# Attention block and two quantised convolutions in one kernel: a new tail for the depthwise stage, and the order of work around four stage borders

## The chip, the core and the metric

The kernel runs on one core of a Trainium2 chip. The metric is the device time of one execution in microseconds (us). Engines are written as in the profile: PE (TensorE matmul), PEld (its weight loads), DVE (VectorE), ACT (ScalarE), POOL (GpSimd), SP (SyncE, which here only issues DMAs). Lines such as L684 are lines of the kernel before; lines of the changed kernel are called so where they are used.

## What is computed

The input x is 4 images of 128 channels and 128 x 128 pixels. The reference, cut to its steps:

```
tok = overlapping 16 x 16 regions of x, step 14          # 9 x 9 regions per image
y = layernorm(tok); q, k, v = split(y @ w_qkv)            # 4 heads of 32
o = softmax(q k^T / sqrt(32)) v
tok = o @ w_out + b_out + tok
xf = overlapped regions, summed and divided by their count
y = layernorm(xf) @ w_p0 + b_p0                           # 256 channels
y = depthwise 5x5 conv(y); batchnorm; gelu; gelu
x = y @ w_p2 + b_p2 + xf
a = quant4(x); c = conv3x3(a, quant4(w1)); batchnorm
a = quant4(c); c = conv3x3(a, quant4(w2)); batchnorm
out = c + x
```

Batch norm takes its mean and variance over all images, so the stages behind it can't start before the stage ahead has ended everywhere.

## The kernel before

**Attention stage.** The 36 bands (4 images x 9 rows of regions) are the outer loop, `for t in range(T)` at line 872; the 9 regions j of a band are the inner one. Each step j issues scores(j) (L684, softmax Exp at L692), values(j-1) (L747, L755, reciprocal at L767), and beside them pieces of other work, listed by `beside(t)` (line 781): the first layer norm of the band after next and its q and k projections (L458), the output projection of the band before (L510), its second layer norm and projection to 256 channels (L526, copied out by ACT at L531), and the depthwise convolution of an image whose bands are done. The lists in `plan` (lines 824 to 834) say which piece stands in which step; bands 0 to 9 use another division of the projections (lines 837 to 841). `left` carries the last four projections of a band into step 0 of the next one. Within this stage the order on PE, ACT, DVE and SP is the order in which the Python code issues (`manual_schedule`, line 867).

A layer norm chunk (`normalise`, line 341) has five pieces: squares (ACT, L351), sums over channels (PE, L357) and variance, `deviation` (ACT: Ln at L371, Exp at L372, then a DMA of the row to DRAM from ACT's queue, L374), `spread` (SP: the row comes back to all partitions, L379), and the product with it (DVE, L388). There are 4 chunks per band, 144 in all. In the plan for bands after the ninth the `deviation` of the four chunks ends steps 0, 2, 4 and 6. Score tiles in PSUM have one buffer each (`ps_s`), and three further buffers (`ps_m`) are shared by the projections and the depthwise products.

**Depthwise convolution.** It is done on PE with banded matrices (L611): 16 output rows at once from 20 input rows, the input read back from DRAM (`y2_d`), the output copied by ACT (L618), its statistics taken by DVE (L622), and stored to DRAM (`cv_d`). The work is cut into units: one for each of the first three images, then 4, 2 and 2 row groups of the last. The first five units run beside the bands. The sixth, called the rest here, runs alone after the last band (lines 891 to 908): 16 steps, loads four steps ahead into 4 buffers, its stores issued from ACT's queue.

**Batch norm of the depthwise output.** Lines 964 to 994: 64 aggregations (L973), products with a mask (L983), 4 sums on PE (L985), scale and shift. This part lies outside the manual order.

**Gelu stage** (`gelu_stage`, line 1087). 64 units of 8 rows: load `cv` and `xf`, three Gelu activations (L1110, L1113), projection (L1122), sum and quantisation, and the first 3x3 convolution two units later (L1064), which keeps the last image's result in SBUF (`c1_s`).

**Last stages** (`last_stages`, line 1178). The same 64 units pass once through Relu, quantisation and the second convolution for its statistics (two units later), where the last image's results are kept in `c1_s`, and the first three images' units once more to write the output.

ACT's functions come from tables that have to be loaded. One line at the start asks for the set that has Ln and Exp:

```
nc.scalar.preload_act_table_set("natural_log_exp_and_others")   # line 107
```

No other line of the kernel before asks for a set. The program also holds a second, safe copy of all layers behind a branch (`conv_seq_kernel`, line 1246), which runs only if the scores could be too large; with these inputs it does not.

Of the kernel before, what the change touches and what calls it, by code (L numbers as in the profile page):

```python
# [14 lines left out]
P = 128  # L15
# [6 lines left out]
RB = 4  # L22
# [24 lines left out]
def layers(  # L47
# [51 lines left out]

    def vector(v, name):  # L100
        n = v.shape[0] // P
        t = const.tile([P, n], F32, name=name)
        nc.sync.dma_start(out=t, in_=v.rearrange("(h p) -> p h", p=P))
        return t
# [18 lines left out]
    nc.sync.dma_start(out=wo, in_=w_out)  # L123
    bo = vector(b_out, "bo")
    g2, b2 = vector(ln2_g, "g2"), vector(ln2_b, "b2")
    wp0 = const.tile([P, 2, P], F32, name="wp0")
    nc.sync.dma_start(out=wp0, in_=w_p0.rearrange("p (h m) -> p h m", h=2))
    bp0 = vector(b_p0, "bp0")
# [4 lines left out]
    with (  # L133
        tc.tile_pool(name=f"prep_{tag}", bufs=1) as prep,
        tc.tile_pool(name=f"ps_p_{tag}", bufs=1, space=PSUM) as ps_p,
    ):
        center = prep.tile([P, P], F32, name="center")
        nc.vector.tensor_scalar(center, ident, -1.0 / P, None, ALU.add)
        nc.vector.tensor_scalar(wqkv[:, :P], wqkv[:, :P], float(HD) ** -0.5, None, ALU.mult)
        pb = ps_p.tile([P, 8], F32, name="pb")  # L140
        qb = const.tile([P, 1], F32, name="qb")
        nc.tensor.matmul(pb[:, 0:1], wqkv[:, :P], b1, start=True, stop=True)
        nc.vector.tensor_copy(qb, pb[:, 0:1])
        bv = prep.tile([P, 1], F32, name="bv")
        nc.tensor.matmul(pb[:, 1:2], wqkv[:, 2 * P :], b1, start=True, stop=True)
        nc.vector.tensor_copy(bv, pb[:, 1:2])
        nc.tensor.matmul(pb[:, 2:3], wo, bv, start=True, stop=True)
        nc.vector.tensor_tensor(bo, pb[:, 2:3], bo, ALU.add)
        for h in range(2):
            nc.tensor.matmul(pb[:, 3 + h : 4 + h], wp0[:, h, :], b2, start=True, stop=True)  # L150
        nc.vector.tensor_tensor(bp0, pb[:, 3:5], bp0, ALU.add)
        nc.vector.tensor_scalar(wqkv, wqkv, g1, None, ALU.mult)
        nc.vector.tensor_scalar(wp0, wp0, g2, None, ALU.mult)

        for w in (wqkv, wp0.rearrange("p h m -> p (h m)")):
            n = w.shape[1]
            pw = ps_p.tile([P, 3 * P], F32, name="pw")
            nc.tensor.matmul(pw[:, :n], center, w, start=True, stop=True)
            nc.vector.tensor_copy(w, pw[:, :n])
# [10 lines left out]
    st0 = sctx.enter_context(tc.tile_pool(name=f"st0_{tag}", bufs=1)).tile(  # L170
        [P, NCK, 2, 4, len(units), 6], F32, name="st0"
    )


    with ExitStack() as actx:
# [4 lines left out]
        y2p, up, cp = pool("y2p", 1), pool("up", 3), pool("cp", 2)  # L180
# [8 lines left out]
        xp, yp, sums = pool("xp", 2), pool("yp", 2), pool("sums", 1)  # L189
        att, attn_t, attn_v = pool("att", 2 if safe else 4), pool("attn_t", 2), pool("attn_v", 2)  # L190
# [365 lines left out]
        def conv_steps(n, ahead=2, rest=None):  # L556


# [7 lines left out]
            def load(at):  # L566
                k, jj, c = tiles[at]
                if rest:
                    W[k, jj] = rest[0][k][:, :, 8 * jj : 8 * jj + 8, :]
                    ut = rest[1].tile([P, ng * nc_ * CW], F32, name="u")  # L570
                else:
                    if c == 0:
                        W[k, jj] = up.tile([P, 3, 8, 32], F32, name="w")
                        weights(W[k, jj], k, jj, 1, nc.sync.dma_start)
                    ut = up.tile([P, 32 * CW], F32, name="u")[:, : ng * nc_ * CW]
                U[at] = ut = ut.rearrange("p (g c x) -> p g c x", g=ng, c=nc_)
                for half in range(2):
                    ch = 32 * k + 16 * half + 8 * jj + c
                    for a, z in ((0, GR), (GR, GR + 4)):
# [4 lines left out]
                            in_=bass.AP(  # L584
                                y2_d[b].tensor,
                                y2_d[b][GR * g0 + a, 0, ch, 0:1].offset,
                                [[2 * P * CW, 2 * (z - a)], [GR * 2 * 2 * P * CW, ng], [1, nc_ * CW]],
                            ),
                        )

            def products(at):
                k, jj, c0 = tiles[at]
                ut, wt = U.pop(at), W[k, jj]
                if rest:
                    sc = ps_s.tile([P, 2, 2, NT], F32, name=f"sc{at % 2}")
                    pc = [
                        sc[:, half].rearrange("p a n -> p (a n)")[:, : nj * ng * CW].rearrange(
                            "p (j g x) -> p j g x", j=nj, g=ng
                        )
                        for half in range(2)  # L600
                    ]
                else:
                    pc = [ps_m.tile([P, nj, ng, CW], F32, name="pm") for _ in range(2)]
                for j in range(nj):

                    for s, (a, z) in ((1, (0, CW)), (0, (1, CW)), (2, (0, CW - 1))):
                        for half in range(2):
                            hs = slice(64 * half, 64 * half + KD)
                            for q in range(4):
                                c = 4 * j + q  # L610
# [29 lines left out]
            for at in range(len(tiles)):  # L640
                def one(at=at):
                    if at + ahead < len(tiles):
                        load(at + ahead)
                    products(at)

                steps.append(one)
            return steps

        def attention(t):

# [639 lines left out]
```

## Time and profile before

| what | us |
|---|---|
| median of 3 runs (lowest, highest) | 3295.52 (3294.91, 3316.36) |
| the profiled execution, its time | 3291.11 |
| its span, first to last instruction | 3289.0 |
| attention stage, by the timeline of PE | 0 to 2219 |
| tail: last projections, the rest, batch norm, first Gelu | 2219 to 2348 |
| Gelu stage and first convolution on PE | 2348 to 2823 |
| second convolution, statistics pass | 2829 to 3091 |
| output pass | 3091 to 3289 |
| PE, DVE, ACT, POOL busy | 94%, 61%, 61%, 25% |

The table's stage borders are read from the timeline. PE's share is high in every stage but the tail, where the page's slices show the granted clock falling to 6 tenths. A busy share is an average: which wait ends last in a stage has to be read from that stage.

### The profile page before, as it was taken

The page shows a single profiled execution, that of the slowest core. Times are in us where ns is not written, and L with a number is a line of the kernel's source. Part 1 is how long each engine was busy: PE and PEld are TensorE (multiplying, and loading weights), DVE is VectorE, ACT ScalarE, POOL GpSimd, SP SyncE. Part 2 cuts the span into 40 slices and gives each one's busy share as a digit, 9 for nine tenths or more (in the row PEclk, how much of TensorE's full clock was granted, in tenths as well). Part 3 has the DMA queues.
Part 4 walks back from the last instruction along what each step waited for, and adds up shares of the span by engine and source line. Part 5 has one row for each costly group of instructions (what it writes and reads, how often), then busy time and mean ns, then how long its engine had stood idle before and what let it go on. Part 6 is the DMA issues. An engine that isn't in the chain of part 4 may idle for free.

```text
span 3289.0 us, 75777 instructions
## 1 busy us (share of the span) xinstructions
PE 3093.5 (94%) x30922; PEld 1541.3 (47%) x30922; DVE 2020.6 (61%) x3247; ACT 1992.0 (61%) x2670; POOL 828.3 (25%) x1042
## 2 busy tenths in 40 slices
PE   7999999999999999999998998884799999999998
PEld 4555554444544444544444444553444444444343
DVE  5777887776766667676555664542455555666543
ACT  5777776777777676777565564532477767333443
POOL 3444443333333333333222222210111111000000
PEclk9999999999999999999999998876699999999999
DMA  3455677888886788886899888766799999452298
GB/s 93 135 172 159 174 181 179 194 211 196 210 198 166 182 205 208 198 211 166 190 202 206 206 192 202 191 169 176 242 356 360 359 357 300 150 167 71 99 359 311
DMA packets 812363, 682.76 MB, mean 208 GB/s; under 512 B 581646, under 2 KB 696679, under 8 KB 812007
## 3 DMA queue, kind: packets, MB, share of 16 engines
q1 hardware_dynamic: 793447, 673.10, 74.8%
q10 hardware_dynamic: 18560, 4.72, 0.6%
q8 instruction: 247, 4.05, 0.5%
q14 instruction: 109, 0.89, 0.1%
HBM read 410.81 MB, written 270.81 MB: 207 GB/s over the span
## 4 chain that ended last, share of the span: by engine, by line
PE 77%; DMA 10%; ACT 5%; DVE 3%; SPq 2%; issue 2%; ACTq 0%; POOL 0%; DVEq 0%; POOLq 0%
PE pc L1064 19%; PE pm L611 9%; PE sc L684 9%; PE po L747 8%; PE pm L458 6%; PE pb L1122 6%; PE pm L526 5%; PE pm L670 4%; PE po L755 4%; DMA y_d<-y 3%; PE pm L510 3%; PE pm L357 3%; DMA xn<-row 2%; DMA cv_d<-c 2%; DMA u<-y_d 2%
## 5 line engine op out<-in xcount | busy, mean ns | idle before, releaser
L767 DVE RECIPROCAL rd<-po 128x256 f32<-128x256 f32 x324 | 569.3, 1757 | 451.2 <-PE po L755 448.3
L1064 PE MATMUL pc<-q,wq 128*128 128x512 fp8e4 x3168 | 702.0, 381 | 14.4 <-DVE q L1076 14.4
L692 ACT ACTIVATE pt<-sc 128x1024 f32<-128x1024 f32 x648 | 628.1, 1025 | 129.3 <-PE sc L684 65.1
L702 POOL TENSOR_TENSOR sm<-pt 128x512 f32<-128x512 f32 x324 | 412.9, 1274 | 1048.1 <-ACT pt L692 706.8
L1064 PEld LDWEIGHTS <-wq 128*128 128x128 fp8e4 x3168 | 309.0, 98 | 417.7 <-issue 50.2
L684 PE MATMUL sc<-q,kr 32*128 32x256 f32 x5184 | 405.1, 415 | 20.3 <-ACT pt L692 20.1
L611 PE MATMUL pm<-u,w 40*32 40x504 f32 (+5 forms) x7680 | 369.1, 504 | 33.8 <-DMA u<-y_d 20.8
L684 PEld LDWEIGHTS sc<-q,kr 32*128 32x128 f32 x5184 | 250.1, 190 | 259.3 <-issue 166.1
L747 PE MATMUL po<-pt,v 128*32 128x256 f32 x5184 | 361.5, 398 | 8.7 <-DVE part L771 7.7
L618 ACT COPY c<-pm 128x512 f32<-128x512 f32 (+1 forms) x256 | 132.0, 563 | 264.4 <-PE pm L611 254.4
L622 DVE BATCH_NORM_STATS2 st<-c 128x6 f32<-128x512 f32 (+2 forms) x384 | 174.6, 505 | 190.1 <-ACT c L618 189.5
L526 PE MATMUL pm<-xn,wp 128*128 128x512 f32 (+1 forms) x576 | 249.7, 565 | 37.2 <-ACT y L531 20.0
L531 ACT ACTIVATE y<-pm,bp 128x512 f32<-128x512 f32 (+1 forms) x288 | 183.0, 641 | 146.1 <-DMA y_d<-y 80.3
L458 PE MATMUL pm<-xn,wqkv 128*128 128x512 f32 (+1 forms) x576 | 251.5, 565 | 11.6 <-DVE xn L388 9.0
L702 DVE TENSOR_TENSOR sm<-pt 128x512 f32<-128x512 f32 x324 | 243.5, 751 | 29.7 <-ACT pt L692 29.5
L611 PEld LDWEIGHTS pm<-u,w 40*32 40x32 f32 x7680 | 145.2, 112 | 216.8 <-issue 161.4
L1122 PE MATMUL pb<-cv,wp 128*128 128x512 f32 x512 | 232.6, 598 | 11.4 <-ACT cv L1113 11.4
L747 PEld LDWEIGHTS po<-pt,v 128*32 128x32 f32 x5184 | 139.6, 111 | 182.7 <-issue 108.7
L1072 DVE BATCH_NORM_STATS2 st<-pc 128x6 f32<-128x512 f32 x256 | 165.6, 689 | 67.3 <-PE pc L1064 67.3
L755 PE MATMUL po<-sm,ones 128*32 128x256 f32 x2592 | 206.0, 390 | 0.0
L670 PE MATMUL pm<-wqkv,yr 128*128 128x128 f32 x1296 | 193.4, 290 | 0.0
L670 PEld LDWEIGHTS pm<-wqkv,yr 128*128 128x128 f32 x1296 | 159.0, 192 | 68.7 <-issue 44.4
(147 smaller groups left out, 3410.8 us busy)
## 6 DMA issues: line engine op xcount, KB each, us to landing
cv<-cv_d SPq DMA_DIRECT2D x64, 1024.0 KB
u<-y_d SPq DMA_DIRECT2D x224, 256.0 KB
cv_d<-c SPq DMA_DIRECT2D x192, 256.0 KB
xn<-row SPq DMA_DIRECT2D x80, 512.0 KB
y_d<-y SPq DMA_DIRECT2D x160, 256.0 KB
xfl<-xf_d SPq DMA_DIRECT2D x64, 512.0 KB
id_d<-y SPq DMA_DIRECT2D x64, 512.0 KB
idt<-id_d SPq DMA_DIRECT2D x64, 512.0 KB
```

Source lines behind the costliest of these rows:

```text
L458: nc.tensor.matmul(pm[:, : n * P], wqkv[:, m * P : (m + 1) * P], held["xn"][hh], start=True, stop=True,)
L526: nc.tensor.matmul(pm[:, : n * P], wp0[:, h, :], held["xn"][hh], start=True, stop=True)
L611: nc.tensor.matmul(pc[half][32 * q : 32 * q + 32, j, :, a:z], wt[hs, s, c0 + c, :], ut[hs, :, c, a + s - 1 : z + s - 1], start=(s == 1), s ...
L670: nc.tensor.matmul(pv[:, m, c, :], region(yr, j + m)[:, c * P : (c + 1) * P], wqkv[:, 2 * P :], start=True, stop=True,)
L684: nc.tensor.matmul(sc[h // 2][:, h % 2, kc, :].rearrange("p (r c) -> p r c", c=RS), region(kr, j)[hs, kc * P : (kc + 1) * P], queries(j, h ...
L692: nc.scalar.activation(pt, sc[p], AF.Exp)
L702: add(sm, pt[:, :, 0, :], pt[:, :, 1, :], ALU.add)
L747: nc.tensor.matmul(po[hs, 0, :], v[:, kc, hs], pt[h // 2][:, h % 2, kc, :], start=(kc == 0), stop=(kc == 1),)
L755: nc.tensor.matmul(po[hs, 1, :], ones, sm[h // 2][:, h % 2, :], start=True, stop=True)
L767: nc.vector.reciprocal(rd, po[:, 1, :])
L1064: nc.tensor.matmul(pc[:, h], w[:, t, :], q1[b][:, r + dy : r + dy + RB, dx : dx + P], start=(t == 0), stop=(t == 8),)
L1122: nc.tensor.matmul(pb[:, m], wp2[:, h, :], cv[:, h, px], start=(h == 0), stop=(h == 1))
```

## The change

It has six parts.

1. **Start.** x is loaded before all weights that the first layer norm doesn't need; the preparation of the weights is cut in two functions, which run between the pieces of the first layer norm. All small vectors share one tile.
2. **Carried projection split.** Of the four projections in `left`, two stay in step 0 and two go to step 2, but for the last image when a new convolution unit begins. A new unit's steps stand later in their band (`where`).
3. **Tail.** The rest of the depthwise convolution is a function of its own (`conv_rest`): 8 steps of a whole channel chunk (4 x 4 x 3 x 4 products), all inputs and weights held in tiles of their own, weights loaded from POOL's queue, part of the inputs loaded early, stores on SP's and ACT's queues. The pools `up` and `cp` close with the bands.
4. **Statistics.** The aggregations come chunk by chunk inside the rest. The block after it is now in manual order, has one product in place of eight, and asks for the Gelu table set at its head.
5. **Gelu stage.** `cv` of two units is loaded before `xf`; the first unit's Gelus go in two halves.
6. **Second convolution.** It runs three units behind its quantisation, not two, and the first unit is quantised in two halves.

The diff, cut to its core:

```diff
+    vectors, used = const.tile([P, 24], F32, name="vectors"), [0]
...
-        t = const.tile([P, n], F32, name=name)
+        t = vectors[:, used[0] : used[0] + n]
+        used[0] += n
...
-    nc.sync.dma_start(out=wo, in_=w_out)
-    bo = vector(b_out, "bo")
-    g2, b2 = vector(ln2_g, "g2"), vector(ln2_b, "b2")
...
-    nc.sync.dma_start(out=wp0, in_=w_p0.rearrange("p (h m) -> p h m", h=2))
-    bp0 = vector(b_p0, "bp0")
...
+    def prepare_qkv(pb, pw, center):
...
+    def prepare_rest(pb, pw, center):
...
+    mvp = stp.tile([P, 2, NCK * 2 * 4], F32, name="mvp")
+
+    def chunk_stats(k):
+        flat = st0[:, k].rearrange("p a j n s -> p (a j) (n s)")
+        for m in range(8):
+            nc.vector.bn_aggr(mvp[:, :, 8 * k + m], flat[:, m, :])
...
+        up, cp = pool("up", 3), pool("cp", 2)
...
+        def depthwise(outs, wt, ut, n):
...
+        def conv_rest(n, w_t, u_t, c_t):
+            b, g0, ng = units[n]
+            early = 5
+            at = GR + 2
...
+            U = [u_t.tile([P, ng, 16, CW], F32, name=f"u{k}") for k in range(NCK)]
+            W = [w_t.tile([P, 3, 16, 32], F32, name=f"w{k}") for k in range(NCK)]
+            for k in range(NCK):
+                weights(W[k], k, 0, 2, nc.gpsimd.dma_start)
+            for k in range(early):
+                load(k, 0, at, 0, 1)
...
+            def step(k):
+                sc = ps_s.tile([P, 2, 2, NT], F32, name=f"sc{k % 2}")
...
+                depthwise(pc, W[k], U[k], 16)
+                for half in range(2):
+                    cv = c_t.tile([P, 4, ng, CW], F32, name=f"c{half}")
+                    nc.scalar.copy(
...
+                    engine = (nc.sync, nc.scalar)[half]
...
+            def run_all():
+                for k in range(4):
+                    late(k)
+                for k in range(NCK):
+                    step(k)
+                    chunk_stats(k)
+                    if k + 4 < NCK:
+                        late(k + 4)
...
-            for j in sorted((1, 3, 5, 7, 8, 4, 6, 2, 0)[: len(conv)]):
+            where = (3, 5, 7, 8, 4, 6, 1, 2, 0) if fresh else (1, 3, 5, 7, 8, 4, 6, 2, 0)
+            for j in sorted(where[: len(conv)]):
...
+            f0, f1 = (f, []) if fresh and bands[t - 2][0] == B - 1 else (f[:2], f[2:])
...
-                ([a1[1]], [], f, [*c[0], a1[2]]),
+                ([a1[1]], [], f0, [*c[0], a1[2]]),
...
-                ([a2[1]], [a1[4]], b1[:2], [*c[2], a2[2]]),
+                ([a2[1]], [a1[4]], [*f1, *b1[:2]], [*c[2], a2[2]]),
...
+            bctx.close()
+            pools = [actx.enter_context(tc.tile_pool(name=f"late{n}_{tag}", bufs=n)) for n in (1, 2)]
+            run(left)
+            left.clear()
+            flush(len(stores))
...
+            rest = conv_rest(len(units) - 1, pools[0], pools[0], pools[1])
             run(beside(T))
             flush(len(stores))
...
+            rest()
...
     with (
+        nullcontext() if safe else tc.manual_schedule(engines=MANUAL),
         tc.tile_pool(name=f"bn0_{tag}", bufs=1) as bn0,
...
+        nc.scalar.preload_act_table_set("gelu_and_others")
...
-            for q in range(4):
-                nc.vector.tensor_scalar(ex[:, :, q], mv[:, m, :], quad[:, q : q + 1], None, ALU.mult)
...
+                for px in (slice(0, U // 2), slice(U // 2, U)) if n == 0 else (slice(0, U),):
...
+            for n in range(2):
+                load_xf(n)
...
-            for n in range(len(units) + 2):
+            for n in range(len(units) + 3):
...
+                    for h in (slice(0, RB), slice(RB, 2 * RB)) if n == 0 else (slice(0, 2 * RB),):
...
-                if n >= 2:
-                    b, k = units[n - 2]
-                    pc = conv3x3(ps_d, n - 2, wq[1])
+                if n >= 3:
+                    b, k = units[n - 3]
+                    pc = conv3x3(ps_d, n - 3, wq[1])
```

## The prediction

> **What bounds the kernel now.** I read the page first (engine shares, slices), then busy time by stage, then ScalarE's groups, then the timeline around single instructions.
>
> ```profile
> PE 3093.5 (94%) x30922; PEld 1541.3 (47%) x30922; DVE 2020.6 (61%) x3247; ACT 1992.0 (61%) x2670; POOL 828.3 (25%) x1042
> ```
>
> ```profile
> 300.00:550.00 250.00, 244.10 (x2536) 126.83 (x2535) 201.71 (x297) 184.20 (x274) 107.05 (x129) 0.99 0.67 171
> ...
> 1300.00:1580.00 280.00, 276.90 (x3215) 139.24 (x3208) 194.07 (x301) 202.71 (x305) 99.27 (x126) 1.00 0.80 193
> ```
>
> Columns: span, then busy PE, weight loads, DVE, ACT, POOL, clock, DMA. TensorE (PE) is the bound of the attention stage (0 to 2219 us), 98% busy, but ScalarE (ACT) stands right behind it with 72 to 74%, and the two hand work back and forth in every step. Only the tail, 2219 to 2348 us, leaves PE idle and at half clock.
>
> ```profile
> L371 ACT ACTIVATE rstd<-rstd,eps_t 128x256 f32<-128x256 f32 (+1 forms) x144 | 69.8, 484 | 24.2 <-DVE rstd L367 22.5 <-issue 1.1 <-ACT rstd L372 0.6
> ...
> L372 ACT ACTIVATE rstd<-rstd 128x256 f32<-128x256 f32 (+1 forms) x144 | 56.6, 393 | 4.6
> ...
> L1110 ACT ACT_TABLE_LOAD x1 | 1.3, 1283 | 10.0 <-DMA xfl<-xf_d 10.0
> ```
>
> L371 is Ln, L372 Exp: one pair for each of 144 layer-norm chunks. Before, there are two table loads in the whole run (L107 at the start, L1110 at the first Gelu), 1.283 us each.
>
> **The finding that decides.** The change adds a preload of the Gelu set in front of the tail's statistics (line 1050 after). In the instruction list of the changed program it does not stand there. It is ACT's second instruction, right behind the first preload, and from then on every Ln and every following Exp has its own load:
>
> ```
> 1 L110 LoadActFuncSet
> 2 L1050 LoadActFuncSet
> 3 L355 Activation sq<-xt 128x1024 x2
> ...
> 1410 L375 LoadActFuncSet
> 1411 L375 Activation rstd<-rstd,eps_t 128x256 [waits DVE_49]
> 1412 L376 LoadActFuncSet
> 1413 L376 Activation rstd<-rstd 128x256 [waits Activation_49]
> ```
>
> 144 and 144 in this program, where the list of the program before has none there (and its two loads are the two in the trace). The softmax Exps (L692) find their set loaded by L376. The first Gelu still has its own load.
>
> **What the Trainium skill says.** ScalarE: Activation LUTs, "Table sets: the hidden batching unit": Ln and Exp share natural_log_exp_and_others, so one load serves both; the trace before agrees, with one load for 144 pairs. The same page, "What ACT_TABLE_LOAD costs": 1283 ns for any set, plus about 1380 ns of drain, 2.66 us a switch. The trace agrees on 1283; the Gelu after it starts 0.02 us later (2342.30 + 1.28, next at 2343.60), and ACT had stood idle before it, so a drain is not seen here. TensorE: Matmul & The Clock Gate, "Part 1: The HAM clock gate": PE runs at half clock until it has been busy for a window. The trace agrees (below).
>
> **Part 1, the loads.** Two per chunk: 2 x 1.283 = 2.57 us of ACT time, 288 x 1.283 = 370 us in all. From both sides: 0 if ACT's idle time takes them all; 2 x 2.66 = 5.3 us a chunk by the skill's price. I take 2.57, as the one row of before shows no drain. An early band:
>
> ```profile
> 252.22 0.51 ACT L371 ACTIVATE rstd<-rstd,eps_t 128x256 f32<-128x256 f32 x1
> 252.76 0.42 ACT L372 ACTIVATE rstd<-rstd 128x256 f32<-128x256 f32 x1
> 253.21 0.48 ACTq L374 DMA_DIRECT2D row<-rstd  x1
> 253.79 1.94 ACT L692 ACTIVATE pt<-sc 128x1024 f32<-128x1024 f32 x2 [0.61 <-ACT rstd L372]
> ```
>
> ```profile
> 254.09 1.56 PE L510 MATMUL pm<-ob,wo 128*128 128x384 f32 x4
> 255.57 1.34 PE L684 MATMUL sc<-q,kr 32*128 32x256 f32 x16
> ```
>
> The two softmax Exps end at 255.73; the next scores at 255.57 write the same two score tiles (one buffer each), so PE may not start them before. With the loads the Exps end at 258.3, and PE waits about 1.9 us more. What is queued behind the load on ACT: Exp, the row DMA, both softmax Exps; who waits: scores, then everything on PE. In a step with a depthwise product (L611, 2.8 us) PE comes 1.3 us later and the wait shrinks, often to nothing.
>
> I laid 2.57 us on each of the 144 places in ACT's timeline, took off every wait of ACT that follows, and compared the end of the Exps with the next scores. Bands 0 to 9 (no depthwise work): 1.9, 1.7, 1.25 and 0 us for a band's four chunks, 50 us together, 30 of 42 places over 1.2. 545 to 1590 us: 52, mostly 1.77 in step 0 of a band and 0.5 in one other. 1590 to 2219: 22. The split of the carried projection takes two y copies (0.58 each) and their DMA waits out of step 0, before its Ln, so I take 18 off the second figure and 7 off the third. Sum 50 + 34 + 15 = 99 us.
>
> Such stalls also cost clock:
>
> ```profile
> 532.09 0.70 PE L684 MATMUL sc<-q,kr 32*128 32x256 f32 x4 [1.52 <-ACT pt L692]
> 533.00 1.32 PE L684 MATMUL sc<-q,kr 32*128 32x256 f32 x12 [0.21 <-ACT pt L692]
> 534.26 1.93 PE L747 MATMUL po<-pt,v 128*32 128x256 f32 x16
> 535.97 1.08 PE L755 MATMUL po<-sm,ones 128*32 128x256 f32 x8
> ```
>
> After 1.5 us of waiting L747 takes 1.93 instead of 1.07, and the step runs 2.1 us longer. Waits of 1.3 to 1.4 us for DVE (at 77.7, 159.7, 1619.0 us) show no such fall, so I take half, 1.1 us, on some 50 stalls over 1.2 us: 55 us (bounds 0 and 105). The row DMA leaves 2.6 us late too; SyncE's queue waits for it (324 us in 101 waits now), and the normalising DVE product waits for the spread in 31 of 144 cases: 8 us (0 to 25). Loads: 99 + 55 + 8 = 162.
>
> **Part 2, the start.** x is issued 2.9 us earlier (six DMAs move behind it on SP); the first layer norm's two pairs put 2.6 and 5.1 us on the chain to the first projection. Net +2 (-3 to +3).
>
> **Part 3, the tail.** The last conv unit has 16 steps from 2263.5 to 2330, each starved by loads and stores; PE at 0.50 clock. It becomes 8 steps of 192 products on full chunks, with u and w held and stores on two queues. The rate while fed is 5.29/184 = 28.7 ns, at half clock: 8 x 5.5 = 44 instead of 67, -23; at full clock (1.58 us for 96) 8 x 3.2 = 26, -40; bounded by its 7.8 MB at 254 GB/s (173 GB/s at a DMA share of 0.68), 31 us; if loads starve it still, -8. I take -23. Weights on POOL's queue: POOL is idle there. Early u loads stand before the last spreads on SP and share the DMAs; with the loads' 5 us the last y comes +1. Statistics by chunk: nothing, they already ran between the products (L973); 8 aggregations now end it instead of 4 (+0.8), one product for eight (-0.9). The first cv load no longer waits for the last stores (it waits for w and PE): the first Gelu waits for the shift (6.5 us after the last statistics) and not for cv (10.7 us), -4. The first Gelu unit in halves lets PE start 2 us earlier. xf behind cv is in that. Sum -28 (-45 to -8).
>
> **Part 4, the second convolution.**
>
> ```profile
> 3043.03 4.07 PE L1064 MATMUL pc<-q,wq 128*128 128x512 fp8e4 x18 [0.83 <-DVE q L1076]
> ...
> 3087.13 13.18 PE L1064 MATMUL pc<-q,wq 128*128 128x512 fp8e4 x60 [0.83 <-DVE q L1076]
> ```
>
> Between these, units take 4.90 us instead of 3.91: product, statistics, copy, Relu, quantising, next product go in a ring. A third unit of distance breaks it: 10 x 1.0 = -10; first unit in halves -1. All four PSUM buffers are free for it. Splits and moved conv steps in three bands: -4 for waits on y stores (0 to -15).
>
> **Sum.** 162 + 2 - 28 - 11 - 4 = +121 on the profiled 3291.1 us (span 3289.0): 3412. The median of the runs is 4.4 us above: 3416.
>
> **Rivals.** (a) ACT's idle time, 26 to 28% of the stage, takes most of the loads, and the change is not slower. The place is the step after each Ln; it decides at 43/144 = 0.30 us a chunk. For: 59 of 144 places do show 0. Against: in the first ten bands ACT would go from 74% to 95% of the same time (184 + 5.1 x 8 x 1.283 of 250). Time 3245 to 3330, likeliest 3320. Chance 0.11. (b) Each switch costs the skill's 2.66 us: the same count on ACT's timeline gives 451 us, with some 130 stalls x 1.1, minus 43: about 3840. For: the skill; against: the 0.02 us after the load. 0.09. (c) The loads do not run, and the change does only what its text says: 3291 - 43 - 5 = 3243 with the start. 0.03. (d) Stalls feed each other (every one drops the clock, late spreads hold DVE): +60 to +170 more, 3480 to 3580. 0.09. Mine: 0.68, own range 3340 to 3480.
>
> **Chances.** Range 3320 to 3580: it holds mine, (d) and the upper end of (a), and leaves out (b), (c) and most of (a). About 1% is what a measurement can tell: faster by over 1% (below 3262) from (c) and the low end of (a), 0.05; within, 0.08; slower 0.87.
>
> **What would show it.** In the profile after: 291 table loads on ACT, mean near 1.28 us (2.66 with the gaps would be (b)); ACT share up by 11 points; PE idle "<-ACT pt" at the scores from 20 us to about 100; bands 0 to 9 longer by 6 to 9 us each, later ones by 2 to 4; softmax Exps following the row DMA. Tail from last scores to first second projection about 100 us instead of 128; stalls of 0.83 gone near 3043 to 3087. Wrong if bands keep their length with the loads there (a), or if the loads are absent (c).

## The result, and the profile after

The changed kernel takes 3581.98 us (median of four runs, 3574.72 to 3590.2), the kernel before on the same chip 3297.88: ratio 1.084, with an interval of 1.0815 to 1.0867. The forecast was 3416, with 3580 as the upper end of its range. So the direction and the cause were forecast, and the loss, 284 us by the medians, came out 2.4 times as large as the 118 forecast.

The profiled execution has a span of 3588.4 us, 299.4 more than before. Three pieces of the PE timeline say where. The first is the attention stage, from the start to the last scores: 2511.2 us, before 2204.2, so +307. The second is the tail, from there to the first second projection: 142.2, before 143.8. The third is all after that: 935.1, before 941.0. The forecast had +160, -28 and -11.

The page's row of busy time, to be held against the first fence of the prediction:

```profile
PE 3253.9 (91%) x30922; PEld 1602.2 (45%) x30922; DVE 2058.7 (57%) x3242; ACT 2366.9 (66%) x2947; POOL 835.8 (23%) x1058
```

PE makes the same 30922 products, but is busy 160 us longer with them. ACT has 375 us more, and 277 more instructions (289 table loads, less 12 others). The groups of ACT that answer to L371 and L372 of before (name, count, busy time and mean, idle time ahead):

```profile
L375 ACT ACT_TABLE_LOAD x144 | 184.8, 1283 | 4.2 <-issue 1.1 <-ACT rstd L376 0.6
L376 ACT ACT_TABLE_LOAD x144 | 184.8, 1283 | 2.6
...
L375 ACT ACTIVATE rstd<-rstd,eps_t 128x256 f32<-128x256 f32 (+1 forms) x144 | 69.8, 484 | 1.7
L376 ACT ACTIVATE rstd<-rstd 128x256 f32<-128x256 f32 (+1 forms) x144 | 56.5, 393 | 1.6
...
L1050 ACT ACT_TABLE_LOAD x1 | 1.3, 1283 | 0.0
L1199 ACT ACT_TABLE_LOAD x1 | 1.3, 1283 | 4.9 <-DMA cv<-cv_d 4.9
```

All 291 loads are there at 1.283 us each, and the preload of line 1050 runs 2.0 us into the trace, as the second of them. Ln and Exp take what they took before. The first Gelu still has its own load (L1199), so the preload saves nothing even there. Two stretches in bands of the same kind as those shown of before (columns as there):

```profile
300.00:550.00 250.00, 226.58 (x2072) 116.00 (x2072) 170.42 (x247) 193.34 (x259) 88.50 (x111) 0.92 0.51 138
1400.00:1680.00 280.00, 265.82 (x2968) 131.59 (x2949) 178.69 (x270) 220.06 (x304) 91.61 (x117) 0.96 0.79 180
```

In the first, ACT goes from 184 to 193 of 250 us while PE issues 2072 products instead of 2536: ACT does not fill up, PE starves. The clock falls from 0.99 to 0.92. The group of the scores, L684 of before and L753 of after:

```profile
L684 PE MATMUL sc<-q,kr 32*128 32x256 f32 x5184 | 405.1, 415 | 20.3 <-ACT pt L692 20.1
```

```profile
L753 PE MATMUL sc<-q,kr 32*128 32x256 f32 x5184 | 486.2, 438 | 159.8 <-ACT pt L761 159.7
```

The idle time ahead of the scores, put down to the softmax Exp, goes from 20 to 160 us; about 100 was forecast. One such place, in band 22: ACT first, then PE.

```profile
1416.81 0.58 ACT L535 ACTIVATE y<-pm,vectors 128x384 f32<-128x384 f32 x1 [1.93 <-DMA y_d<-y]
1417.68 0.58 ACT L535 ACTIVATE y<-pm,vectors 128x384 f32<-128x384 f32 x1 [0.30 <-DMA y_d<-y]
1418.28 1.28 ACT L375 ACT_TABLE_LOAD   x1
1419.57 0.51 ACT L375 ACTIVATE rstd<-rstd,eps_t 128x256 f32<-128x256 f32 x1
1420.10 1.28 ACT L376 ACT_TABLE_LOAD   x1
1421.39 0.42 ACT L376 ACTIVATE rstd<-rstd 128x256 f32<-128x256 f32 x1
1421.84 0.48 ACTq L378 DMA_DIRECT2D row<-rstd  x1
1422.43 1.94 ACT L761 ACTIVATE pt<-sc 128x1024 f32<-128x1024 f32 x2 [0.61 <-ACT rstd L376]
```

```profile
1423.50 0.70 PE L753 MATMUL sc<-q,kr 32*128 32x256 f32 x4 [2.44 <-ACT pt L761]
1424.42 1.31 PE L753 MATMUL sc<-q,kr 32*128 32x256 f32 x12 [0.21 <-ACT pt L761]
1425.65 1.93 PE L816 MATMUL po<-pt,v 128*32 128x256 f32 x16
1427.36 1.08 PE L824 MATMUL po<-sm,ones 128*32 128x256 f32 x8
```

From the start of the load to the start of Ln it is 1.29 us, and over all 288 loads ACT idles only 6.8 us ahead of them: no drain, so rival (b) is out. PE waits 2.44 us, and then L816 takes 1.93 instead of 1.07. Note the first line: the two y copies that are left in this step stand ahead of the load and wait 1.93 us for a store. In the whole stage, 80 scores wait like this, 59 of them over 1.2 us, together 55 us in bands 0 to 9, 77 in bands 10 to 27 and 27 in the rest; before, it was 1, 8 and 11 us, with 5 waits over 1.2.

Not every wait costs clock. Step 6 of bands 4 and 5 waits the same time, and only in band 4 the products behind it are slow:

```profile
298.73 2.99 PE L753 MATMUL sc<-q,kr 32*128 32x256 f32 x16 [1.91 <-ACT pt L761]
301.65 1.94 PE L816 MATMUL po<-pt,v 128*32 128x256 f32 x16
```

```profile
360.21 0.70 PE L753 MATMUL sc<-q,kr 32*128 32x256 f32 x4 [1.92 <-ACT pt L761]
361.12 1.13 PE L753 MATMUL sc<-q,kr 32*128 32x256 f32 x12 [0.21 <-ACT pt L761]
362.18 1.07 PE L816 MATMUL po<-pt,v 128*32 128x256 f32 x16
```

Behind 48 of the 59 waits over 1.2 us the next L816 group takes more than 1.5 us, behind the other 11 it does not. All changes of the granted clock in this trace lie on a fixed grid of 3.41 us, so it may matter where a wait falls against that grid; that is not shown.

The second convolution, with five waits of 0.83 where before had ten:

```profile
3366.66 4.06 PE L1147 MATMUL pc<-q,wq 128*128 128x512 fp8e4 x18 [0.83 <-DVE q L1159]
...
3381.35 4.07 PE L1147 MATMUL pc<-q,wq 128*128 128x512 fp8e4 x18 [0.83 <-DVE q L1159]
3386.25 94.12 PE L1147 MATMUL pc<-q,wq 128*128 128x512 fp8e4 x433 [0.83 <-DVE q L1159]
```

### The profile page after: what moved, and what is told of

The parts are those of the page before. It is cut to its first block, busy times and chain, and to the rows that moved or that the text cites. A ratio compares the mean times of both kernels' runs of the same rounds, so it can differ in the third digit from the quotient of the medians.

```text
span 3588.4 us, 75971 instructions
## 1 busy us (share of the span) xinstructions
PE 3253.9 (91%) x30922; PEld 1602.2 (45%) x30922; DVE 2058.7 (57%) x3242; ACT 2366.9 (66%) x2947; POOL 835.8 (23%) x1058
## 4 chain that ended last, share of the span: by engine, by line
PE 66%; ACT 13%; DMA 8%; issue 8%; DVE 2%; SPq 2%; ACTq 1%; POOL 0%; DVEq 0%; POOLq 0%
PE pc L1147 18%; PE sc L753 8%; PE po L816 7%; PE pb L1211 6%; PE pm L569 6%; PE pm L462 5%; PE pm L530 4%; PE pm L739 4%; ACT pt L761 4%; ACT L375 3%; PE po L824 3%; DMA y_d<-y 3%; PE pm L361 3%; PE pm L514 2%; DMA xn<-row 1%
## 5 line engine op out<-in xcount | busy, mean ns | idle before, releaser
L753 PE MATMUL sc<-q,kr 32*128 32x256 f32 x5184 | 486.2, 438 | 159.8 <-ACT pt L761 159.7
L753 PEld LDWEIGHTS sc<-q,kr 32*128 32x128 f32 x5184 | 287.5, 199 | 439.0 <-ACT pt L761 295.8
L569 PE MATMUL pm<-u,w 40*32 40x504 f32 (+5 forms) x7680 | 386.6, 512 | 64.7 <-DMA u<-y_d 24.6
L771 DVE TENSOR_TENSOR sm<-pt 128x512 f32<-128x512 f32 x324 | 279.7, 863 | 225.1 <-ACT pt L761 224.2
L816 PE MATMUL po<-pt,v 128*32 128x256 f32 x5184 | 399.7, 432 | 4.3 <-DVE part L840 3.3
L535 ACT ACTIVATE y<-pm,vectors 128x512 f32<-128x512 f32 (+1 forms) x288 | 182.5, 641 | 150.9 <-PE pm L530 80.2
L816 PEld LDWEIGHTS po<-pt,v 128*32 128x32 f32 x5184 | 147.0, 118 | 201.1 <-issue 108.3
L824 PE MATMUL po<-sm,ones 128*32 128x256 f32 x2592 | 221.5, 416 | 0.0
L620 DVE BATCH_NORM_STATS2 st<-c 128x6 f32<-128x512 f32 (+2 forms) x320 | 160.5, 547 | 106.1 <-ACT c L616 105.7
```

Of the source, the lines that this page charges most:

```text
L569: nc.tensor.matmul(outs[half][32 * q : 32 * q + 32, j, :, a:z], wt[hs, s, c, :], ut[hs, :, c, a + s - 1 : z + s - 1], start=(s == 1), stop ...
L753: nc.tensor.matmul(sc[h // 2][:, h % 2, kc, :].rearrange("p (r c) -> p r c", c=RS), region(kr, j)[hs, kc * P : (kc + 1) * P], queries(j, h ...
L771: add(sm, pt[:, :, 0, :], pt[:, :, 1, :], ALU.add)
L816: nc.tensor.matmul(po[hs, 0, :], v[:, kc, hs], pt[h // 2][:, h % 2, kc, :], start=(kc == 0), stop=(kc == 1),)
L824: nc.tensor.matmul(po[hs, 1, :], ones, sm[h // 2][:, h % 2, :], start=True, stop=True)
```

## The experiments

Each ratio is to the kernel before on the same chip, whose median differed a little from one group of runs to the next (3292.5 to 3305.1), with its interval in brackets. A microsecond behind a ratio is the run's median.

**Without the preload: are the loads the whole loss?** The changed kernel less one line:

```
-        nc.scalar.preload_act_table_set("gelu_and_others")
```

> The changed kernel without the line that asks for the Gelu set: one table load at the start, one at the first Gelu. Theory A, the 288 loads are the whole loss and the other edits gain: bands as short as before or shorter, and about 3250 us (3298 less 40 to 50), ratio 0.985. Rival, part of the loss comes from the rewritten tail or the moved steps: 3300 us or more.

Measured 0.998 [0.9969, 0.9991], 3299.82 us. Two table loads are left. One line is worth 8.6 points of ratio, some 283 us, and what the rest of the change gains is next to nothing, not the 41 us that the forecast gave it. The attention stage is longer than before even so: bands 28 to 34 take 568 us instead of 543.

**The preload alone.** The kernel before with that line and nothing else:

```
+        nc.scalar.preload_act_table_set("gelu_and_others")
```

> The kernel before with only the line that asks for the Gelu set, at the head of its statistics: 288 loads appear between Ln and Exp. Theory A: the bands grow by the 305 us by which they grew in the change, so about 3600 us, ratio 1.09. Rival, the moved projections and conv steps made the loads dearer than they are by themselves: 3480 us or less.

Measured 1.0888 [1.0859, 1.0917], 3596.77 us, with 144 and 144 loads at Ln and Exp. The line alone makes the whole loss. Why the compiler, with a second preload at the front, no longer lets Ln and Exp share a set is not shown by any run.

**Is it the table, or ScalarE's time?** The version without the preload, with two copies of a tile onto itself (600 elements, 0.69 us each) ahead of each Ln and of each Exp in place of a load (`idle_t` is a tile of later statistics, reserved early for this):

```
+                nc.scalar.copy(idle_t, idle_t)
+                nc.scalar.copy(idle_t, idle_t)
                 nc.scalar.activation(rstd, rstd, AF.Ln, bias=eps_t)
+                nc.scalar.copy(idle_t, idle_t)
+                nc.scalar.copy(idle_t, idle_t)
                 nc.scalar.activation(rstd, rstd, AF.Exp, scale=-0.5)
```

> The changed kernel without the Gelu preload, and two ScalarE copies of 600 elements (about 0.64 us each) in the place of each of the 288 loads; the copies go to a tile that nothing uses at that time. If a load costs just its 1.28 us of ScalarE time: as the change, 3560 to 3600 us. If a switch of tables costs more than its own row (a drain, slower Exps after it): 3480 us or less.

Measured 1.0705 [1.0675, 1.0735], 3537.49 us, between the two forecasts: 238 of the 283 us come back with no table load in sight. What counts is time on ScalarE at this place. The missing 45 us are not all the loads' own. The copies add less work: ACT's busy time is 349 us above the version without the preload (2337.7 against 1988.4), with the loads 378 (2366.9). From the end of the instruction ahead to the end of Exp it is 3.51 us with the loads and 3.32 with the copies, in the mean of 144 chunks. By the price found below for the second half of the copies, 140 us for 166 us of work, the 29 us of missing work would be worth some 25 (an estimate). The 20 that remain are little more than the uncertainty of the two runs.

**The same copies behind the row DMA.** All four copies stand after the row is sent, so that only the softmax Exp is late:

```
                 nc.scalar.dma_start(out=row[:, :w], in_=rstd[0:P:32, :])
+                nc.scalar.copy(idle_t, idle_t)
+                nc.scalar.copy(idle_t, idle_t)
+                nc.scalar.copy(idle_t, idle_t)
+                nc.scalar.copy(idle_t, idle_t)
```

> As the run with copies for the loads, but all four copies stand behind the row DMA: the softmax Exps are as late as there, the row and its spread are not late. If only the softmax Exps matter: within 20 us of that run. If the late row, on which SyncE's queue waits, is part of the loss: 60 us or more under it.

Measured 1.0614 [1.0584, 1.0644], 3509.48 us, again between the two forecasts. The late row costs about 28 us of the 238: VectorE waits 89 us for the row's return in place of 111. The other 210 us remain when only what stands behind the row on ScalarE is late, the softmax Exps first of all.

**Filling the waits: how much is the slow clock?** The changed kernel with unread products on TensorE ahead of the scores that waited, by a table of places made from the profile after:

```
+                    filler = ps_o.tile([P, 2, NT], F32, name="po") if FILL.get((t, j)) else None
+                    for _ in range(FILL.get((t, j), 0)):
+                        nc.tensor.matmul(
+                            filler.rearrange("p a n -> p (a n)")[:, : 3 * P], ident, wqkv,
+                            start=True, stop=True,
+                        )
                     last = lambda j=j, values=values: values(j)
```

> The changed kernel, table loads included, with products nobody reads (128x384, 0.39 us each, written to the po tile) put on TensorE ahead of the 80 scores that waited for the softmax Exp, each as many as its wait was long (357 in all, 139 us). ScalarE's work is untouched. Theory (half of the loss is the slow clock that follows each wait): the waits for pt shrink from 160 us to under 50, the granted clock of the attention stage comes back from 0.92 to 0.96 or more, the products after the wait take 1.07 and not 1.93 us, and the time falls by 100 to 170 us, to 3410 to 3480. Rival (ScalarE's own chain sets the pace, and the slow products only fill time that TensorE would wait anyway): the clock comes back, but the time stays within 30 us of 3582.

Measured 1.0831 [1.0808, 1.0854], 3570.8 us, at first sight the rival's case. The stretch up to the last scores says otherwise (first line after, second this run):

```profile
0.00:2520.00 2520.00, 2270.24 (x25478) 1142.85 (x25481) 1509.50 (x2341) 1834.98 (x2498) 751.45 (x955) 0.92 0.68 162
```

```profile
0.00:2509.00 2509.00, 2371.82 (x26160) 1220.32 (x26162) 1507.34 (x2341) 1835.93 (x2498) 753.39 (x955) 0.97 0.67 163
```

```profile
L1011 PE MATMUL po<-wqkv,ident 128*128 128x384 f32 x714 | 268.7, 525 | 55.7 <-DVE part L876 37.8 <-DVE ob L874 18.0
```

The fillers took 268.7 us (each f32 product is two entries, 0.75 us together, where I had counted 0.39) and waited 55.7 us for VectorE to read the po tile: 324 us put into waits of 160. Without them PE's own work is 2371.8 - 268.7 = 2103 us, 167 less than after and the same as before (2105, below). So all of PE's additional busy time goes when the waits are filled, but the fillers took about as much as came back. The run is inconclusive as to time. A second one has fewer.

> As the run with filled waits, with the fillers counted anew. In that run each product of 128x384 took 0.75 us and not 0.39, and began up to 2.5 us late, because it waits for VectorE to read the po tile; fillers and their waits were 324 us where 160 were to be filled. Now 108 products stand in 64 places, one to five in each, cut so that they end before the softmax Exp does. Theory (half of the loss is the slow clock after each wait; in that run TensorE's own work shrank by 158 us): the granted clock of the attention stage is 0.95 or more and the time falls to 3420 to 3500. Rival (ScalarE's chain sets the pace): the clock comes back in the same way and the time stays above 3550.

```profile
0.00:2213.00 2213.00, 2104.94 (x25414) 1080.93 (x25414) 1470.66 (x2341) 1463.52 (x2212) 752.33 (x955) 0.97 0.77 185
```

```profile
0.00:2446.00 2446.00, 2264.30 (x25667) 1143.26 (x25672) 1506.09 (x2341) 1830.78 (x2498) 753.25 (x955) 0.96 0.69 167
```

The first line is the kernel before, the second this run, both up to the last scores. Measured 1.0658 [1.0636, 1.068], 3510.94 us, 71 less than after (60 by the ratios), with 1831 us of ScalarE's work, as after. The theory's range ended at 3500, so it is a near miss on size, and the rival (above 3550) is out. PE's own work is 2264.3 less 91.5 of fillers, 2173 us, which is 97 less than after. The granted clock bears this out: from the first scores to the last, PE was at half clock for 385 us after and for 197 here. One place shows how:

```profile
319.58 0.88 PE L1011 MATMUL po<-wqkv,ident 128*128 128x384 f32 x2 [0.39 <-DVE ob L874]
320.42 0.70 PE L789 MATMUL sc<-q,kr 32*128 32x256 f32 x4
321.34 1.13 PE L789 MATMUL sc<-q,kr 32*128 32x256 f32 x12 [0.21 <-ACT pt L797]
322.40 1.07 PE L852 MATMUL po<-pt,v 128*32 128x256 f32 x16
```

In the profile after, the same step of the same band has a wait of 1.23 us ahead of the scores, and L816 then takes 1.93. Here the time is taken up by a filler of 0.88, and the product takes 1.07. The scores' own record still has the second half of the wait in it: 0.70 for four entries, then 0.21, where an undisturbed step has one record of 1.15. That is the third piece of the loss: the scores are busy 456.7 us here and 412.4 where the fillers covered everything, 44 us.

With the version without the preload as the yardstick the pieces close. PE's idle time between the first and the last scores is 99 us there and 234 after, 135 more. Its busy time is 2102 there and 2243 after, 141 more, and 97 and 44 make 141. The record of the granted clock gives the size of the second piece by another way: PE was busy at half clock for 148 us there and for 348 after, so if every such product takes twice its time, the slow clock costs 100 us (an estimate).

**Half of the work.** The version with copies, with only the two ahead of the Ln left (the expectation says ahead of the Exp; the kernel that ran has them ahead of the Ln):

```
                 nc.scalar.activation(rstd, rstd, AF.Ln, bias=eps_t)
-                nc.scalar.copy(idle_t, idle_t)
-                nc.scalar.copy(idle_t, idle_t)
                 nc.scalar.activation(rstd, rstd, AF.Exp, scale=-0.5)
```

> The version without the preload that has four copies of 600 elements on ScalarE in each chunk (3537, or 238 above the version without them), with only the two ahead of the Exp left, 1.3 us a chunk in place of 2.6. Theory (each place has some slack, and only what is over it stops TensorE: of the 80 waits in the profile after, 67 of 159 us remain if each is cut by 1.3): less than half of the cost is left, 60 to 110 us above 3300, so 3360 to 3410. Rival (each microsecond on ScalarE costs the same): 119 above, 3420 or more. Second rival (the slow clock has a threshold near 1.2 us of wait, so that short waits cost next to nothing): under 50 above, 3350 or less.

Measured 1.0277 [1.0234, 1.0321], 3389.43 us: 90 above the version without copies, by ratio 98 of the 239. The waits for the Exp are 52.2 us:

```profile
L758 PE MATMUL sc<-q,kr 32*128 32x256 f32 x5184 | 443.9, 423 | 52.9 <-ACT pt L766 52.2
```

The first two copies of a chunk cost 98 us, the second two 140; ACT's busy time grows by 183 us for the first and by 166 more for the second. There is slack, but only a little: even half of the time is mostly paid for. Part of the slack may be that of the place. Ahead of the Ln ACT idled 24 us before, mostly waiting for VectorE, and ahead of the Exp 5; a copy can fill the first and hardly the second.

**Does the split take waits off the loads?** The changed kernel, loads included, with the carried projection and the convolution steps as before:

```
-            where = (3, 5, 7, 8, 4, 6, 1, 2, 0) if fresh else (1, 3, 5, 7, 8, 4, 6, 2, 0)
+            where = (1, 3, 5, 7, 8, 4, 6, 2, 0)
...
-            f0, f1 = (f, []) if fresh and bands[t - 2][0] == B - 1 else (f[:2], f[2:])
+            f0, f1 = f, []
```

> The changed kernel with its table loads, but with the carried projection in one piece in step 0 and the convolution steps in their old places. My prediction took 25 us of waits off the loads because the split takes two copies of y and their waits out of step 0. Theory (that credit was wrong: the first copies of y wait for their store in step 0 either way, and the Ln stands behind them): the time is within 15 us of 3582, or below it by the 11 that the same edit saves without the loads. Rival (the credit holds, 25 us of waits and the slow clock after them): 3600 to 3630, with bands 10 to 27 two us longer each.

Measured 1.082 [1.0782, 1.0857], 3566.03 us, and the waits for the Exp are what they were, 160.0 us:

```profile
L753 PE MATMUL sc<-q,kr 32*128 32x256 f32 x5184 | 483.1, 433 | 160.1 <-ACT pt L761 160.0
```

In sum the credit of 25 us was for nothing. By bands it is uneven: without the split the scores wait 63.5 us in bands 10 to 27 (76.9 with it) and 41.5 us in the bands behind (27.4 with it), each read from one profile. So what the split saved at the end it lost in the middle.

**The same edit without the loads.**

> The changed kernel without the preload, and with the carried projection in one piece in step 0 and the convolution steps in their old places, as in the kernel before. Theory (the split and the moved steps cost the 24 us that bands 28 to 34 take longer): these bands go back to about 543 us together and the time is 20 to 25 us below 3300. Rival (the bands are longer for another reason, such as the order of buffers): the time is within 5 us of 3300. Forecast in my prediction: the split saves 4, so 3304.

Measured 0.9946 [0.9925, 0.9966], 3280.59 us, against 0.998 with the split: 11 us better by ratio, with an uncertainty of about 8. Bands 28 to 34 take 555 us instead of 568 (before 543). So the split and the moved steps cost something where I had them save 4; half of the additional length of these bands has another cause, which stays open.

**The tail.** After, SyncE's queue and PE around the last projection:

```profile
2536.51 16.17 SPq L658 DMA_DIRECT2D u<-y_d x10
2552.78 0.82 SPq L402 DMA_DIRECT2D xf_d<-xf  x2
2553.66 1.97 SPq L383 DMA_DIRECT2D xn<-row  x2
```

```profile
2570.97 9.39 PE L530 MATMUL pm<-xn,wp 128*128 128x512 f32 x16 [34.22 <-DVE xn L392]
...
2588.80 0.65 PE L569 MATMUL sc<-u,w 40*32 40x128 f32 x8 [8.44 <-DMA u<-y_d]
```

Before, the same projection waited 16 us:

```profile
2247.41 8.76 PE L526 MATMUL pm<-xn,wp 128*128 128x512 f32 x16 [16.27 <-DVE xn L388]
```

The ten early loads of u hold SyncE's queue for 16 us ahead of xn, and PE waits 34 us for the projection's input. I moved these loads behind the spread (in the version without the preload, where the wait is 30.4):

```
-            for k in range(early):
-                load(k, 0, at, 0, 1)
...
             def run_all():
+                for k in range(early):
+                    load(k, 0, at, 0, 1)
                 for k in range(4):
                     late(k)
```

> The changed kernel without the preload, and the ten early loads of the last depthwise unit's input issued behind the last spread instead of ahead of it. Theory (these loads stand ahead of xn on SyncE's queue and hold the last projection): TensorE's wait for xn in the tail falls from 30 us to 16 or less, as in the kernel before, and the time is 12 to 20 us below that of the version without the preload (3300), some 3283. Rival (the weights on GpSimd's queue fill the DMA engines, whatever SyncE issues): the wait stays above 25 us and the time within 5 us of 3300. Second rival: the wait shrinks, but the depthwise products wait for their input instead, and the time stays the same.

Measured 0.9971 [0.9961, 0.9982], 3285.25 us: by ratio 3 us better than 0.998, within the uncertainty.

```profile
2242.00:2266.00 24.00, 0.46 (x1) 0.46 (x2) 1.57 (x4) 1.35 (x4) 6.03 (x12) 0.52 0.94 217
```

```profile
2265.54 9.54 PE L530 MATMUL pm<-xn,wp 128*128 128x512 f32 x16 [24.38 <-DVE xn L392]
2289.24 11.16 PE L569 MATMUL sc<-u,w 40*32 40x128 f32 x405 [14.16 <-DMA u<-y_d]
```

Now the DMA engines are busy for a share of 0.94, with the sixteen weight loads on GpSimd's queue, and PE still waits 24 us for xn; and what is won there comes back as a wait for u. The second rival is the nearest. So the weights went back to SyncE's queue, half of them between the products:

```
-            for k in range(NCK):
-                weights(W[k], k, 0, 2, nc.gpsimd.dma_start)
+            for k in range(NCK // 2):
+                weights(W[k], k, 0, 2, nc.sync.dma_start)
...
                     if k + 4 < NCK:
+                        weights(W[k + 4], k + 4, 0, 2, nc.sync.dma_start)
```

> The version with the early u loads behind the spread, and the depthwise weights taken off GpSimd's queue: four chunks on SyncE's queue ahead of the last projection, the other four one step at a time between the products, as in the kernel before. Theory (the sixteen weight loads fill the DMA engines, share 0.94, while xn is spread): TensorE's wait for xn falls from 24 us to 17 or less, the wait for u stays near 14 us or less, and the time is 8 to 14 us below the 3285 of the version with only the u loads moved. Rival (bytes are bytes: the weights only come later, and the depthwise products wait for them): within 4 us of 3285.

Measured 0.9971 [0.9957, 0.9985], 3284.31 us. The wait for xn is 14.0 us, near the 16 of before the change, and the wait for u still 14.5: the rival's number holds. From the last scores to the first second projection the tail takes 136.5 us in the version without the preload and 135.6 and 135.5 in the two runs of this section, so the order of the transfers only decided which product shows the wait. That the bytes are the limit, the rival's reason, is not shown: in the last run the DMA share is 0.61 while PE waits for xn and 0.68 from there until the wait for u ends.

**The second convolution alone.** The kernel before with one edit:

```
-            for n in range(len(units) + 2):
+            for n in range(len(units) + 3):
...
-                if n >= 2:
-                    b, k = units[n - 2]
+                if n >= 3:
+                    b, k = units[n - 3]
```

> The kernel before with one edit, the second convolution three units behind its quantisation instead of two. Theory (product, statistics, copy, Relu and quantising go in a ring of 4.9 us a unit): 8 to 10 us faster than before, ratio 0.997, with the stalls of 0.83 us near 3043 to 3087 gone. Rival (the ring is only the start of the stage, and the extra unit is given back at its end): within 3 us of before.

Measured 0.9977 [0.9965, 0.9988], 3287.39 us, a gain of 7.5 us (4 to 12). Five of the ten waits of 0.83 are gone, and the other five are still there; what ends them in these five units stays open.

**What is left, put together.** Without the preload, without the split, with the tail's weights and loads as in the last tail run:

> The changed kernel without the preload, with the carried projection and the convolution steps as in the kernel before, and the tail's weights and input loads behind the spread: what is left of the change is the start, the eight-step depthwise unit, the statistics by chunk and the second convolution's third unit. Theory (the parts add up): ratio to before 0.990 to 0.993, some 25 to 30 us faster. Rival (the late bands' length is noise of the DMA queues and the tail gives back what it gains): ratio 0.995 or more.

Measured 0.9917 [0.9903, 0.9932], 3268.82 us: faster than both kernels, by some 27 us and 313 us, and within the theory's range.

## Why the prediction was wrong

The cause was right: the preload turns into 288 table loads on ScalarE, at the price read from the row of before. The size failed in the sum for the loads, 162 us where the stage grew by 307. Three terms of that sum failed: the clock was mis-sized (55, measured about 100), the second half of each wait was left out (44), and the raw waits were too small in bands 10 to 27 (34, measured 69). The terms one by one:

- **Raw waits of PE, 99.** They grew by 139.6 us. Bands 0 to 9: 50 forecast, 54 measured. Bands 10 to 27: 34 forecast, 69 measured. Bands 28 on: 15 forecast, 16 measured. The step that failed is "so I take 18 off the second figure and 7 off the third". Taking two y copies out of step 0 leaves two, which in band 22 wait for their store with the Ln behind them. Without the split the waits are the same 160 us. In the last bands the split did save 14 us, twice the 7; in bands 10 to 27 it saved nothing of the 18 and added some 13. Some 15 us of the sum is what the count on ACT's timeline missed.
- **Clock, 55.** The step that failed is "so I take half, 1.1 us, on some 50 stalls". The slow clock cost about 100 us: 97 went when the waits were cut by short products, with ScalarE's work unchanged. That is about 2 us for each of the 48 waits that were followed by slow products. The whole 2.1 us of the one place shown in the prediction, on 48 places, would have been 101. I had halved it on the strength of three waits of 1.3 to 1.4 us for VectorE that show no fall. Waits without a fall do exist, but they are 11 of 59 and not half.
- **The second Exp, no term.** About 44 us is the scores' own record waiting for the second of the two Exps. The prediction has "PE may not start them before" both have ended; its own lines say otherwise, for the scores start at 255.57 and the second Exp ends at 255.73. PE starts behind the first Exp and then waits inside the record, which no column of idle time shows.
- **The rest of PE's work.** Of the 165 us by which PE's work in the stage grew, 22 are there without the loads as well, and so belong to the other edits.
- **Late row, 8 (0 to 25).** About 28 in the run that moved the copies behind the row. It is no further piece; PE shows it in the waits and products above.
- **The drain, rival (b).** The Trainium skill, ScalarE: Activation LUTs, "What ACT_TABLE_LOAD costs", has 1283 ns for a load and about 1380 ns of drain. All 291 loads take 1283 ns; of the drain no run shows a trace, with 1.29 us from load to Ln.
- **Rival (a), ACT's idle time.** Not borne out: half of the work already costs 98 us. ACT has over a quarter of the stage idle, but in the step behind a Ln it stands ahead of PE, and PE's two score tiles allow no lead.
- **Rival (d), stalls feed each other.** Nearest in size (3480 to 3580), and right that the clock matters; but not every stall drops it. That a wait brings on the next was not shown: bands 0 to 9 are 10.4 us longer each on average, bands 10 to 27 7.7 us (2 to 11), without a drift. Both are more than the 6 to 9 and 2 to 4 forecast.
- **Start, +2.** First scores at 35.9 instead of 33.1, +2.7; without the loads 31.2, so the order of loads alone gains 2.
- **Tail, -28.** Measured -1.6, and -7.3 in the version without the loads. The eight steps do take 53 us instead of 67 (-14, forecast -23), but PE waits 18 us more for xn. The prediction saw these loads ahead of the spread and priced it at +1; it costed "Weights on POOL's queue: POOL is idle there" at nothing, but in the run where these loads were in flight with the u loads moved, the DMA engines' share was 0.94 and xn still came 8 us later than before.
- **Second convolution and what follows, -11.** Measured -6.0. The ring loses half of its waits.
- **Split and moved steps, -4.** They cost 11 (about 8 either way).

The Trainium skill, TensorE: Matmul & The Clock Gate, "Part 1: The HAM clock gate", has PE fall to half clock after an idle window of about 3.4 us. The runs show the fall behind single waits of 1.2 to 2.5 us too, though not behind all: in the profile after, all 28 waits over 2 us have it, and 20 of the 31 below. Where half of the copies ran, two waits of 2.1 us did not have it, so this is a count and not a threshold. For pricing a wait here the measurement decides: for those over 1.2 us, about four in five bring some 2 us on top.

## What to carry to other kernels

Look for a table preload in the instruction list, not in the source: if it is hoisted, functions that had shared a set may each get a load of their own. Price a stall of TensorE with three terms, the wait, the products behind it at half clock, and the second half of a paired wait that sits inside the product's own record; here they were about 140, 100 and 44 us. Before giving a credit for moving work out of a step, ask whether what is left there waits for the same thing. Before moving loads to an idle engine's queue, look at the DMA share; here it was 0.94 with sixteen loads on such a queue, and no time was gained.

## What was not expected of the hardware

Short unread products in the waits kept the clock up for longer: 108 of them, 0.85 us each, halved the time at half clock in the attention stage and made the kernel 60 to 71 us faster although they did nothing. The same wait of 1.92 us, in the same step of neighbouring bands, dropped the clock in bands 3, 4 and 7 and left it up in bands 1, 2, 5, 6 and 8. Two copies of 0.69 us took less of ScalarE's time than one load of 1.28: in the traces an activation begins about 0.1 us before the copy ahead of it has ended, where behind a load it begins after the load's end.
